# A graph layer's front reordered: node features, W1 and W3 first, table rows ahead of the dst check, edge attributes behind the rows

## The chip, the cores and the metric

The kernel runs on one core of a Trainium2 chip. The metric is the device time of one execution in microseconds (us); lower is better. A core has five engines that run their own instruction streams: TensorE (PE in the profile, PEld its weight loads), VectorE (DVE), ScalarE (ACT), GpSimd (POOL) and SyncE (SP, which only issues transfers). Transfers are issued by SP, ACT and POOL on queues of their own and are carried by 16 DMA engines that all queues share.

## The reference

1250 nodes have 512 features each: 384 are a vector part (128 channels of 3 components), 128 a scalar part s. 40000 edges, sorted by their target node dst, carry three attributes and a weight r. Two rounds of messages follow, then a residual and a layer norm:

```
x_j = x[src];  v_j, s_j = x_j[:, :384] as (E,128,3), x_j[:, 384:]
s_j = silu(s_j @ W1 + b1) @ W3 + b3
split = s_j * (rbf(r) * cutoff(r) @ W2 + b2)         # 3 x 128
v_msg = v_j * s1 + s3 * edge_attr;   msg = [v_msg, s2]
x1 = x + segment_sum(msg, dst)
... second round: v = x1_j @ U, v_V = v @ V, norms, a two-layer gate, segment_sum over dst
out = layernorm(x + x2)
```

`silu(s @ W1 + b1) @ W3 + b3` and its product with v depend on the node alone, so the kernel computes them once for each of the 1250 nodes, not for each of the 40000 edges.

## The kernel before

Nodes are kept in 10 blocks of 128 rows (NB = 10), shifted by a margin of 8. The edges are cut into 79 chunks of 512, four chunks to a group, 20 groups; a batch is one tile of 128 edges from each of the four chunks of a group, 81 batches in all.

**The front** (lines 118 to 381) loads everything and writes a table `table1` with one row of 640 numbers for each node to HBM. Its order is written out by hand: `manual_schedule` keeps the instructions of each engine in the order of the source. Its steps are:

- Memsets on DVE and POOL, iotas on POOL (`diff`, `part`, `lane`, `half_n`).
- Loads. ACT's queue brings the scalar columns of all nodes (`load_all_nodes`, line 192: blocks 1 to 4, blocks 5 to 8, then blocks 0 and 9 in two pieces each), POOL's queue the other 384 columns (line 203) and then W2, b2, U, V and the second gate's weights. SP's queue brings dst, b3, bu2, W1, b1, W3, weight, src and the edge attributes, in this order. Eight completion semaphores are handed round among the transfers of SP and ACT, and a transfer that takes over one waits until the transfer that had it has landed. Behind its transfers ACT loads its table for silu and runs one element through it (`warm`, line 194).
- The dst check (lines 277 to 290): DVE subtracts from each chunk the start of its window (`local_r`) and takes minimum and maximum, PE adds up the chunks that miss their window into `missed`, and DVE writes `missed_i`. Line 383 loads it into every engine, and a branch picks `windowed` (all chunks fit; taken here) or `general`.
- The layers. `turn_s` transposes the scalar part of four blocks on PE and copies it to `s_t` on DVE; `inner_layer` multiplies with W1 on PE (line 322) and applies silu on ACT. This goes by blocks 0 to 3, 4 to 7, and 8 and 9.
- `split_bias` (line 358) splits a bias into three bf16 parts on DVE, once for b3, once, at the end, for bu2.
- The rows. `make_rows` has PE add the bias and multiply with W3 (lines 336 and 337); `table_row` (line 577) has ACT copy 256 of the 384 results, DVE multiply the node's vector part with the rest (line 579), and SP store the row block (line 584).
- `make_sources` turns src by `by_tile` (four transposes on PE, a copy on ACT) into the index list `src_i` of the gathers.

**The loop** (`windowed`) first turns weight and attributes by `by_tile` and makes the first basis (lines 1459 to 1470). Then it runs the batches. For each, POOL gathers four tiles of 128 table rows by indirect transfers (`gather`, line 739), three batches ahead; the gathers go round five rooms of memory, three in `more`, two in `nodes`. From the fourth batch on the first gather of a batch waits for PE's edge factors two batches earlier. PE makes edge factors (line 854), DVE multiplies rows and factors (`messages`, lines 812 to 883), ACT marks the sources, PE adds the messages up and counts links between nodes. The second round is done by node blocks in between, and an end part normalizes the rows.

The loop's tiles lie in the memory that the front's tiles leave. So POOL's first loop tile, `number` (line 655), waits until the front's last work on DVE is done.

Of the kernel before, what the change touches and what calls it, by code (L numbers as in the profile page):

```python
# [11 lines left out]
F32 = mybir.dt.float32  # L12
# [52 lines left out]
def gnn_resnorm(  # L65
# [64 lines left out]
    rest = n_edges - full * CHUNK  # L130

# [10 lines left out]

    bias_f = front.tile([BIAS_ROWS - 1 + 32, V + 2 * C], F32, name="bias_f")
    nc.vector.memset(bias_f, 0.0)

    unfilled = full // 32 * 32
    nc.vector.memset(sh.att_r[unfilled:, :], 0.0)

# [7 lines left out]


# [4 lines left out]
    load_edges(dst_r, dst)  # L162
    first_last = slice(0, 3, 2)
    three = bias_f.rearrange("(r q) f -> r q f", q=32)[:, 0, :]
    nc.sync.dma_start(three[:, :V], b3.rearrange("(o f) -> o f", o=1).to_broadcast([3, V]))
    for h in range(2):
        nc.sync.dma_start(
            three[:, V + h * C : V + (h + 1) * C],
            bu2.rearrange("(h o c) -> h o c", o=1, c=C)[2 * h].to_broadcast([3, C]),
        )  # L170

    sh.nodes = const.tile([P, NB * width], F32, name="nodes")
    sh.xt = sh.nodes.rearrange("p (b f) -> p b f", f=width)
# [6 lines left out]
    last = n_nodes + MARGIN - (NB - 1) * P  # L180
    warm = const.tile([P, 1], F32, name="warm")
    nc.vector.memset(warm, 0.0)
    nc.vector.memset(sh.xt[last // 32 * 32 :, NB - 1, :], 0.0)
    nc.vector.memset(sh.xt[:MARGIN, 0, :], 0.0)
# [7 lines left out]
    load_all_nodes(nc.scalar, slice(V, width))  # L192

    nc.scalar.activation(warm, warm, AF.Silu)

    diff = front.tile([P, P], I32)
    nc.gpsimd.iota(diff, pattern=[[1, P]], base=0, channel_multiplier=-1)
    nc.gpsimd.memset(sh.src_r[unfilled:, :], 0.0)
    nc.gpsimd.memset(sh.wgt_r[unfilled:, :], 1.0)
    part = numbers([P, 1], [[0, 1]], 0, 1, "part")  # L200
    lane = numbers([P, P], [[1, P]], 0, 0, "lane")
    half_n = numbers([P, N_RBF], [[1, N_RBF]], 1, 0, "half_n")
    load_all_nodes(nc.gpsimd, slice(0, V))

    def load(engine, ap, shape, name):
        t = const.tile(shape, F32, name=name)
        engine.dma_start(t, ap)
        return t

    sh.h_t = const.tile([C, NB * P], F32, name="h_t")
    sh.w1_sb = load(nc.sync, w1, [C, C], "w1_sb")
    sh.b1_sb = load(nc.sync, b1.rearrange("(p o) -> p o", o=1), [C, 1], "b1_sb")

    sh.w3_sb = load(nc.sync, w3, [C, V], "w3_sb")
    load_edges(sh.wgt_r, edge_weight)
    load_edges(sh.src_r.bitcast(I32), src)
    load_edges(sh.att_r, edge_attr, 3)

    w2_sb = const.tile([P, V + CARRY], F32)
    nc.vector.memset(w2_sb, 0.0)
    for i in range(GROUP):
# [12 lines left out]
    sh.b3, sh.bu2 = b3, bu2  # L236


    ident = const.tile([P, P], F32)
    nc.vector.tensor_scalar(ident, diff, 0.0, None, op0=ALU.is_equal)  # L240
    share = front.tile([NCP, 1], F32)
    nc.vector.tensor_scalar(
        share, part[:NCP, :], float(SHARE), float(-MARGIN), op0=ALU.mult, op1=ALU.add
    )
    ones = const.tile([P, P], F32)
    nc.vector.memset(ones, 1.0)
    sh.ones_r = const.tile([BIAS_ROWS, P], BF16, name="ones_r")
    nc.vector.tensor_copy(sh.ones_r, ones[:BIAS_ROWS, :])
    nc.vector.tensor_scalar(half_n, half_n, 0.5, None, op0=ALU.mult)
    sh.ones, sh.ident, sh.lane, sh.part, sh.half_n = ones, ident, lane, part, half_n  # L250


# [9 lines left out]
    nc.vector.tensor_scalar(w2_sb[:, V:], lane[:, :CARRY], own, None, op0=ALU.is_equal)  # L262
# [13 lines left out]

    local_r = front.tile([NCP, CHUNK], F32)
# [10 lines left out]
    missed = ps_front.tile([1, 1], F32)  # L288
    nc.tensor.matmul(missed, misses, ones[:NCP, 0:1], start=True, stop=True)
    nc.vector.tensor_copy(missed_i, missed)  # L290


    sh.carried = fields.tile([P, NGR, TPC * CPG, CARRY], F32, name="carried")
    sh.attr, sh.local = sh.carried[:, :, :, :3], sh.carried[:, :, :, 3]
    sh.weight = fields.tile([P, NGR, TPC * CPG], F32, name="weight")
    sh.src_i = fields.tile([P, NGR, TPC * CPG], I32, name="src_i")
    sh.src_f = fields.tile([P, NGR, TPC * CPG], F32, name="src_f")

    def by_tile(ps, t, col, per, to, bufs=2):
        tp = ps.tile([P, TPC, P], F32, name="tp", bufs=bufs)  # L300
        view = t.rearrange("c (i e k) -> c i e k", i=TPC, k=per)
        for i in range(TPC):
            nc.tensor.transpose(tp[:, i, :NCP], view[:, i, :, col], ident[:NCP, :NCP])
        nc.scalar.copy(
            to.rearrange("p g (i j) -> p i g j", i=TPC),
            tp[:, :, :NCP].rearrange("p i (g j) -> p i g j", j=CPG),
        )


    s_ts = []  # L310

    def turn_s(b0, n):
        tp = ps_front.tile([P, 4 * P], F32, name="xs", bufs=2)
        for b in range(n):
            nc.tensor.transpose(tp[:, b * P : (b + 1) * P], sh.xt[:, b0 + b, V:], ident)
        s_t = front.tile([C, 4 * P], F32, name="s_t", bufs=3)
        nc.vector.tensor_copy(s_t[:, : n * P], tp[:, : n * P])
        s_ts.append(s_t)

    def inner_layer(s_t, b0, n):  # L320
        hp = ps_front.tile([C, 4 * P], F32, name="pp", bufs=4)
        nc.tensor.matmul(hp[:, : n * P], sh.w1_sb, s_t[:, : n * P], start=True, stop=True)
        nc.scalar.activation(
            sh.h_t[:, b0 * P : (b0 + n) * P], hp[:, : n * P], AF.Silu, bias=sh.b1_sb
        )

    sh.by_tile = by_tile
    by_tile(ps_front, local_r, 0, 1, sh.local, 1)
    sh.table1 = tc.dram_tile([NB * P, V + 2 * C], F32, name="table1")
    sh.table2 = tc.dram_tile([NB * P, width], F32, name="table2")  # L330

    def make_rows(b0, n):
        row = sh.rooms[b0 // 4]
        for b in range(b0, b0 + n):
            pp = ps_front.tile([P, 4 * P], F32, name="pp", bufs=4)[:, :V]
            nc.tensor.matmul(pp, sh.ones_r, sh.bias[:, :V], start=True, stop=False)
            nc.tensor.matmul(
                pp, sh.h_t[:, b * P : (b + 1) * P], sh.w3_sb, start=False, stop=True
            )
            table_row(nc, sh, pp, b, row[:, b - b0, :])  # L340

    def make_sources(step):
        if step == 0:
            nc.vector.tensor_scalar(
                sh.src_r, sh.src_r.bitcast(I32), float(MARGIN), None, op0=ALU.add
            )
            return
        by_tile(ps_front, sh.src_r, 0, 1, sh.src_f, 1)
        nc.vector.tensor_copy(sh.src_i, sh.src_f)

    spans = [(b0, min(4, NB - b0)) for b0 in range(0, NB, 4)]
    for span in spans[:-1]:
        turn_s(*span)
    inner_layer(s_ts[0], *spans[0])

    sh.bias = const.tile([BIAS_ROWS, V + 2 * C], BF16, name="bias")

    def split_bias(cols):
        left = bias_f[:BIAS_ROWS, cols]
        nc.vector.tensor_copy(sh.bias[:, cols], left)  # L360
# [1516 lines left out]
```

## Time and profile before

| | us |
|---|---|
| median of 3 runs | 502.84 |
| the three runs | 499.98, 502.84, 510.46 |
| the profiled execution | 500.5 |
| its span, first to last instruction | 498.7 |
| busy in it: DVE | 441.4 |
| PE | 410.5 |
| ACT | 369.1 |
| POOL | 348.6 |

A profile's times count from the start of the span. A line of the timeline has start, duration, engine (SPq, ACTq, POOLq are issues of transfers), line of the kernel, operation, and what is written from what; an x and a number behind it count merged instructions, whose duration is then the whole stretch; brackets hold the idle time ahead of it and what ended it. A line of the groups has count, busy us, mean ns of one, and idle time ahead with its releasers. A line of the queues has packets, MB and the share of the 16 DMA engines' time. What ended an idle time is inferred: of several things waited for the one that came last is named, and where that had long been done it was another, often a transfer.

### The profile page before, as it was taken

The numbers are of one execution on the slowest core, as the hardware profiler recorded it, in microseconds if no ns is written. First come the engines' busy times: TensorE is split into PE (matmuls) and PEld (weight loads), VectorE is DVE, ScalarE is ACT, GpSimd is POOL, SyncE is SP. The second block draws the span as 40 slices with busy tenths as digits, with TensorE's granted clock in tenths as the row PEclk, the third lists the DMA queues.
The fourth block names the chain that finished last, engine by engine and source line by source line (L and its number), as shares of the span: only waits on it lengthen the run. The fifth ranks groups of instructions, "written<-read, shape, count | busy, mean of one in ns | idle before, by whom it ended". The sixth has DMA issues, their size and how long they took to land. (4 is left out here: it accounts for less than half of the span.)

```text
span 498.7 us, 11033 instructions
## 1 busy us (share of the span) xinstructions
PE 410.5 (82%) x4193; PEld 226.0 (45%) x4193; DVE 441.4 (89%) x698; ACT 369.1 (74%) x941; POOL 348.6 (70%) x369
## 2 busy tenths in 40 slices
PE   2946777886889876898899799989979989998991
PEld 1522333353445344454445445544544554545780
DVE  6789998989988998999899799999978989987693
ACT  1436776597778979677898688998978798873573
POOL 6457777777777777777777777777776777655910
PEclk9966887999988999898999799999979999999996
DMA  8768888888888878888988988888887898889023
GB/s 244 252 219 248 256 264 253 263 288 265 263 252 293 258 227 300 252 246 256 297 293 241 312 255 284 294 285 294 263 288 242 270 293 283 272 258 344 2 107 109
DMA packets 38323, 126.96 MB, mean 255 GB/s; under 512 B 6689, under 2 KB 8239, under 8 KB 38259
## 3 DMA queue, kind: packets, MB, share of 16 engines
q0 software_dynamic: 26016, 104.86, 66.9%
q1 hardware_dynamic: 10910, 20.64, 11.8%
q10 hardware_dynamic: 1332, 0.64, 0.5%
q8 instruction: 35, 0.57, 0.4%
q14 instruction: 30, 0.24, 0.2%
HBM read 114.78 MB, written 11.34 MB: 253 GB/s over the span
## 5 line engine op out<-in xcount | busy, mean ns | idle before, releaser
L745 POOL DMA_INDIRECT more<-table,src_i x189 | 186.4, 986 | 59.6 <-issue 49.1
L745 POOL DMA_INDIRECT nodes<-table,src_i x124 | 124.3, 1002 | 42.3 <-issue 32.9
L845 ACT ACTIVATE one<-one,weight,src_f 128x128 f16<-128x128 f16 x313 | 128.5, 482 | 0.5 <-DVE magic L723 0.2
L854 PE MATMUL eb<-w_sb,basis_t 25*128 25x388 f32 x626 | 80.6, 574 | 55.3 <-DVE more L868 33.1
L835 ACT ACTIVATE one<-number,low 128x128 f16<-128x128 f16 x313 | 99.7, 392 | 4.2 <-PE adj L925 3.5
L868 DVE TENSOR_TENSOR more<-more,eb 128x1536 f32<-128x1536 f32 (+2 forms) x49 | 82.8, 1691 | 0.0
L865 DVE TENSOR_TENSOR more<-more,eb 128x1024 f32<-128x1024 f32 (+2 forms) x49 | 57.7, 1179 | 9.4 <-DMA more<-table,src_i 9.2
L854 PEld LDWEIGHTS eb<-w_sb,basis_t 25*128 25x128 f32 x626 | 26.4, 191 | 76.4 <-DVE more L868 45.1
L900 PE MATMUL agg<-more,hot 128*32 128x512 f32 (+1 forms) x378 | 58.8, 679 | 0.0
L868 DVE TENSOR_TENSOR nodes<-nodes,eb 128x1536 f32<-128x1536 f32 (+1 forms) x32 | 54.4, 1699 | 0.0
L907 PEld LDWEIGHTS agg<-more,spread 128*32 128x32 f32 x1134 | 35.9, 117 | 35.8 <-issue 35.5
L865 DVE TENSOR_TENSOR nodes<-nodes,eb 128x1024 f32<-128x1024 f32 (+1 forms) x32 | 37.9, 1185 | 7.1 <-DMA nodes<-table,src_i 6.8
L907 PE MATMUL agg<-more,spread 128*32 128x128 f32 x1134 | 43.8, 284 | 0.0
L823 DVE TENSOR_TENSOR spread<-hot,eb 128x384 f32<-128x384 f32 (+1 forms) x81 | 43.3, 535 | 0.0
L883 DVE TENSOR_TENSOR pair<-number,column 128x640 f16<-128x640 f16 (+1 forms) x81 | 38.7, 479 | 0.0
L925 PE MATMUL adj<-pair,one 128*128 128x160 f16 x313 | 35.8, 236 | 0.0
L900 PE MATMUL agg<-nodes,hot 128*32 128x512 f32 x248 | 34.9, 619 | 0.0
L812 DVE TENSOR_TENSOR hot<-lane,eb 128x128 f32<-128x128 f32 (+1 forms) x81 | 22.6, 280 | 13.2 <-PE eb L854 12.4
L805 ACT COPY basis_t<-work 128x512 f32<-128x512 f32 x20 | 11.7, 585 | 28.4 <-PE work L800 28.4
L907 PEld LDWEIGHTS agg<-nodes,spread 128*32 128x32 f32 x744 | 22.5, 111 | 19.9 <-issue 19.9
L925 PEld LDWEIGHTS <-one 128*128 128x128 f16 x313 | 19.9, 98 | 16.2 <-issue 14.7
L907 PE MATMUL agg<-nodes,spread 128*32 128x128 f32 x744 | 27.0, 274 | 0.0
(258 smaller groups left out, 689.9 us busy)
## 6 DMA issues: line engine op xcount, KB each, us to landing
table<-more SPq DMA_DIRECT2D x10, 320.0 KB, 2.4
spilled<-begun SPq DMA_DIRECT2D x12, 256.0 KB
more<-table,src_i POOLq DMA_INDIRECT x189
more<-spilled SPq DMA_DIRECT2D x2, 1280.0 KB
resid<-h_t SPq DMA_DIRECT2D x9, 256.0 KB, 4.2
node_x<-in_x_dram SPq DMA_DIRECT2D x8, 256.0 KB, 5.3
nodes<-table,src_i POOLq DMA_INDIRECT x124
nodes<-in_x_dram POOLq DMA_DIRECT2D x2, 768.0 KB
```

The costliest lines, as they stand in the source:

```text
L745: got = nc.gpsimd.indirect_dma_start(out=rows_t[:n, j, :], out_offset=None, in_=sh.table1, in_offset=bass.IndirectOffsetOnAxis(ap=sh.src_i ...
L812: nc.vector.tensor_tensor(hots[t][:m, js, :], lane[:m, None, :WIN].to_broadcast(shape), eb[:m, js, V + 3 : V + 4].to_broadcast(shape), op= ...
L823: nc.vector.tensor_mul(spread[t][:m, js], hots[t][:m, js, None, :].to_broadcast(shape), eb[:m, js, V : V + 3, None].to_broadcast(shape),)
L835: nc.scalar.activation(onehots[t][:, j, :], number[:, :P], AF.Abs, bias=low[:, e : e + 1])
L845: nc.scalar.activation(one, one, AF.Relu, scale=less[:, e : e + 1], bias=worth[:, e : e + 1])
L854: made = nc.tensor.matmul(eb[:, j, : V + CARRY], turned[g][rows, i, :], sh.w2_sb[rows, :], start=True, stop=True,)
L865: nc.vector.tensor_mul(msg[:m, js, V:], msg[:m, js, V:], eb[:m, js, C:V])
L868: nc.vector.tensor_mul(msg[:m, js, :V].rearrange("p t (k c) -> p t k c", k=3), msg[:m, js, :V].rearrange("p t (k c) -> p t k c", k=3), eb[ ...
L883: nc.vector.tensor_tensor(pair[:m, js, :].rearrange("p t (l h) -> p t l h", h=2), number[:m, : PARTS * WIN].rearrange("p (l h) -> p l h", ...
L900: nc.tensor.matmul(agg[j * WIN : (j + 1) * WIN, :], hots[t][:m, j, :], msg[:m, j, :width], start=(i == 0), stop=False, skip_group_check=True,)
L907: nc.tensor.matmul(agg[j * WIN : (j + 1) * WIN, c * C : (c + 1) * C], spread[t][:m, j, c, :], msg[:m, j, width:], start=False, stop=(i == ...
L925: nc.tensor.matmul(to[:, :, at : at + WIN], one[:m, j, :], pair[:m, j, :].rearrange("e (p n) -> e p n", n=WIN), start=(i == 0 and j == js[ ...
```

## The change

- SP's order is W1, b1, b3, W3, dst, bu2, src, weight; then the ten row blocks are stored; the attributes load behind them.
- POOL starts its node loads ahead of the memset for weight, `lane` and `half_n`; the attributes' memset moves from DVE to POOL, behind the loads.
- `turn_s` takes blocks 1 to 4, 5 to 8, and 0 and 9, and its copy runs on ACT. `inner_layer` runs for blocks 1 and 2, then 3 and 4, then 5 to 8, then 0 and 9.
- The first bias split comes ahead of DVE's small work on `half_n`, `place` and `sel`.
- Rows are made as 1, 2; 3, 4, 5; 6; 7, 8; and 0, 9, with the layers between them. src and the dst check come on DVE behind row 8 and ahead of rows 0 and 9; `missed_i`, `src_i`, the last columns of `w2_sb` and the second bias split follow.

`split_bias` is called `part_bias` now, otherwise unchanged. The loop is the same, instruction for instruction. The diff, cut:

```diff
+    warm = const.tile([P, 1], F32, name="warm")
+    nc.vector.memset(warm, 0.0)
     bias_f = front.tile([BIAS_ROWS - 1 + 32, V + 2 * C], F32, name="bias_f")
     nc.vector.memset(bias_f, 0.0)
-    nc.vector.memset(sh.att_r[unfilled:, :], 0.0)
...
-    load_edges(dst_r, dst)
+    diff = front.tile([P, P], I32)
+    nc.gpsimd.iota(diff, pattern=[[1, P]], base=0, channel_multiplier=-1)
+    part = numbers([P, 1], [[0, 1]], 0, 1, "part")
+    nc.gpsimd.memset(sh.src_r[unfilled:, :], 0.0)
...
     load_all_nodes(nc.scalar, slice(V, width))
     nc.scalar.activation(warm, warm, AF.Silu)
+    load_all_nodes(nc.gpsimd, slice(0, V))
+    sh.w1_sb = load(nc.sync, w1, [C, C], "w1_sb")
+    sh.b1_sb = load(nc.sync, b1.rearrange("(p o) -> p o", o=1), [C, 1], "b1_sb")
...
+    nc.sync.dma_start(three[:, :V], b3.rearrange("(o f) -> o f", o=1).to_broadcast([3, V]))
+    sh.w3_sb = load(nc.sync, w3, [C, V], "w3_sb")
+    load_edges(dst_r, dst)
...
+    load_edges(sh.src_r.bitcast(I32), src)
...
     nc.gpsimd.memset(sh.wgt_r[unfilled:, :], 1.0)
+    nc.gpsimd.memset(sh.att_r[unfilled:, :], 0.0)
+    load_edges(sh.wgt_r, edge_weight)
     lane = numbers([P, P], [[1, P]], 0, 0, "lane")
     half_n = numbers([P, N_RBF], [[1, N_RBF]], 1, 0, "half_n")
...
+    def turn_s(blocks):
+        tp = ps_front.tile([P, 4 * P], F32, name="xs", bufs=2)
+        for k, b in enumerate(blocks):
+            nc.tensor.transpose(tp[:, k * P : (k + 1) * P], sh.xt[:, b, V:], ident)
+        n = len(blocks) * P
+        s_t = front.tile([C, 4 * P], F32, name="s_t", bufs=3)
+        nc.scalar.copy(s_t[:, :n], tp[:, :n])
+        return s_t[:, :n]
...
+    first_s, next_s = turn_s((1, 2, 3, 4)), turn_s((5, 6, 7, 8))
+    inner_layer(first_s[:, : 2 * P], (1, 2))
+    inner_layer(first_s[:, 2 * P :], (3, 4))
+    part_bias(slice(0, V))
...
+    make_rows((1, 2))
+    inner_layer(next_s, (5, 6, 7, 8))
+    make_rows((3, 4, 5))
+    rest_s = turn_s((0, 9))
+    make_rows((6,))
+    inner_layer(rest_s, (0, 9))
+    make_rows((7, 8))
+    nc.vector.tensor_scalar(sh.src_r, sh.src_r.bitcast(I32), float(MARGIN), None, op0=ALU.add)
+    by_tile(ps_front, sh.src_r, 0, 1, sh.src_f, 1)
     local_r = front.tile([NCP, CHUNK], F32)
     nc.vector.tensor_scalar(local_r, dst_r, share, None, op0=ALU.subtract)
...
+    make_rows((0, 9))
     nc.tensor.matmul(missed, misses, ones[:NCP, 0:1], start=True, stop=True)
     nc.vector.tensor_copy(missed_i, missed)
+    nc.vector.tensor_copy(sh.src_i, sh.src_f)
+    load_edges(sh.att_r, edge_attr, 3)
     by_tile(ps_front, local_r, 0, 1, sh.local, 1)
+    nc.vector.tensor_scalar(w2_sb[:, V:], lane[:, :CARRY], own, None, op0=ALU.is_equal)
+    part_bias(slice(V, V + 2 * C))
```

More of the change, by code (lines that the diff above doesn't have):

```diff
@@ L299, in by_tile @@
[L299 to L318, printed above, removed]
@@ L332, in make_rows @@
[L332 to L349, printed above, removed]
```

170 lines of the change are left out of this document (82 added, 88 removed).

## The prediction

> **What bounds the kernel now.** I read the page first, then the gather line with who waits for it, then the timeline of the first 45 us, because every edit lies ahead of the first message.
>
> ```profile
> span 498.7 us, 11033 instructions
> L745 POOL DMA_INDIRECT more<-table,src_i x189 | 186.4, 986 | 59.6 <-issue 49.1
> L745 POOL DMA_INDIRECT nodes<-table,src_i x124 | 124.3, 1002 | 42.3 <-issue 32.9
> ```
> ```profile
> L745 POOL DMA_INDIRECT more<-table,src_i x189: 918/946/1802, 31.0 to 433.7; - x189
> L745 POOL DMA_INDIRECT nodes<-table,src_i x124: 942/946/1805, 47.0 to 442.1; - x124
> ```
>
> The 313 gathers start at 31.0 and the last at 442.1. They are busy 310.7 us and idle 101.9 us, of which 82.0 is "issue", POOL's own gap between gathers. So POOL waits only some 20 us for others in 412: the loop is a chain of gathers, and a first gather that comes x earlier moves the end by about x. DVE moves along if its own start moves too. The end of the front (lines up to 381) therefore sets the gain.
>
> ```profile
> 25.22 1.47 DVE L579 TENSOR_TENSOR more<-nodes,pp 128x384 f32<-128x384 f32 x2 [0.18 <-ACT more L578]
> 27.99 0.42 DVE L365 TENSOR_TENSOR bias<-bias_f,bias 1x256 bf16<-1x256 f32 x1
> 28.54 0.33 POOL L655 IOTA number<- 128x256 f16 x1 [9.40 <-DVE bias L365]
> 31.05 1.05 POOL L745 DMA_INDIRECT more<-table,src_i  x1 [0.58 <-ACT carried L304]
> 34.66 0.69 DVE L788 TENSOR_TENSOR basis<-turn,fade 128x320 f32<-128x320 f32 x1
> 39.40 0.29 DVE L812 TENSOR_TENSOR hot<-lane,eb 128x128 f32<-128x128 f32 x1
> ```
>
> The last two table rows end on DVE at 26.69. The bias split behind them ends at 28.41 (27.99 + 0.42), 1.72 later, and that releases POOL: its first loop tile starts at 28.54 and the first gather 2.64 us after the split. I call that end F; here F = 28.41. DVE's first message follows 11.0 us after F. Both hang on F, not on the landing of the table.
>
> What comes ahead of the rows:
>
> ```profile
> 1.74 3.96 ACTq L413 DMA_DIRECT2D nodes<-in_x_dram  x4
> 2.09 0.52 POOL L199 MEMSET counts<- 16x512 f32 x1
> 3.06 1.77 POOL L407 DMA_DIRECT2D nodes<-in_x_dram  x2
> 5.74 1.28 ACT L194 ACT_TABLE_LOAD   x1 [5.74 <-DVE row_i L254]
> 7.03 0.20 ACT L194 ACTIVATE warm<-warm 128x1 f32<-128x1 f32 x1
> 9.52 0.19 PE L289 MATMUL missed<-ones,misses 80*1 80x1 f32 x2 [9.52 <-DVE misses L284]
> 13.03 3.51 PE L322 MATMUL pp<-s_t,w_sb 128*128 128x512 f32 x4 [0.89 <-DMA w_sb<-in_L_gnn_W_dram]
> 18.01 3.11 DVE L579 TENSOR_TENSOR more<-nodes,pp 128x384 f32<-128x384 f32 x4 [0.79 <-DMA w_sb<-in_L_gnn_b_dram]
> ```
>
> PE's first work waits 9.52 us for the dst check, its first layer waits for W1 until 13.03, and the first row is multiplied at 18.01. Those waits are what the edits remove.
>
> **The change, part by part.** Clock times below are on the scale of this execution.
>
> *Loads.* W1, b1, b3, W3 go first on SP's queue, ahead of dst; bu2, src and weight follow. W1 is then issued first of all, beside ACT's loads and before POOL's traffic, so it is no longer what the layer waits for. The dst check's 9.52 goes too: PE's first work is the transposes.
>
> *What is late next: ACT.* s_t is now copied by ACT, behind its DMA issues, the table load and warm. Those end at 7.23 (7.03 + 0.20) and were covered while PE waited; now they lie on the path. ACT's last issue (to 5.70) waits for node blocks 5 to 8 to land. POOL's loads of the other 384 columns move ahead of L199's memset and two iotas, by some 0.8 us (2.09 to 3.06, less one small iota that stays), so their data come that much earlier, into the tail of that load:
>
> ```profile
> q10 hardware_dynamic: 804, 0.40, 37.1%
> ```
> ```profile
> q10 hardware_dynamic: 1200, 0.59, 45.9%
> q0 software_dynamic: 13, 0.06, 15.7%
> ```
> ```profile
> q0 software_dynamic: 354, 1.50, 83.6%
> q1 hardware_dynamic: 4, 0.00, 0.1%
> ```
>
> These are the queues from 0 to 4 us, from 0 to 5, and from 5 to 10. ACT's queue (q10) had moved 0.40 MB at 4 us and 0.59 at 5; POOL's (q0) began just before 5. From 5 to 10 POOL's queue moved 354 packets and SP's (q1) four. A POOL packet holds an engine 0.19 us (83.6% of 16 engines for 5 us, over 354). Starting near 4 us, POOL finds about 0.19 MB of 512-byte packets left, some 23 for each engine. Call ACT's delay d. Lower end 0: they finish undisturbed. Upper end: one POOL packet ahead of each, 23 x 0.19 = 4.4 us for what took 1, d = 3.4. I take 1.7, the middle, which is nearest to one POOL load going in between (768 KB at 1.50 MB per 354 packets are 181, 11 for each engine, 2.1 us).
>
> The Trainium skill's DMA: Bandwidth & Descriptors, section "Queues, rings and completion order", says that each engine goes round robin between the queues, a packet at a time. By fair turns SP would not have had 4 packets against 354, so this trace doesn't bear out fair turns; taken literally here it gives the upper end, 3.4.
>
> *Layers and rows.* The prices:
>
> ```profile
> L322 PE MATMUL pp<-s_t,w_sb x6: 377/938/1193, 13.0 to 20.1; 128*128 128x512 f32 x4, 128*128 128x256 f32 x2
> L315 PE MATMUL xs<-ident,nodes x10: 273/421/422, 10.2 to 16.5; 128*128 128x128 f32 x10
> 17.41 0.33 PE L336 MATMUL pp<-bias,ones_r 65*128 65x384 bf16 x1
> 17.57 0.81 PE L337 MATMUL pp<-w_sb,h_t 128*128 128x384 f32 x2
> 17.60 0.37 ACT L578 COPY more<-pp 128x256 f32<-128x256 f32 x1 [0.34 <-PE pp L337]
> L805 ACT COPY basis_t<-work 128x512 f32<-128x512 f32 x20 | 11.7, 585 | 28.4 <-PE work L800 28.4
> ```
>
> PE starts at about half speed: a transpose took 421 ns early and 273 at 16.4, and a 512-column pass 0.88 early (3.51 / 4) against 0.43 by the later rows. For a row costs 0.81 there ((3.11 - 0.67) / 3 on DVE, which PE feeds), 0.16 of it the bias pass (17.41 to 17.57), which leaves 0.65 for two passes of 384. PE was fast 3.3 us after it began unbroken work at 13.03. A slow row is estimated at twice, 1.62. The Trainium skill, in TensorE: Matmul & The Clock Gate, Part 1, tells of a free-running window of some 3.4 us that must be busy before the clock opens, which agrees, and by which the point can fall up to one window later; that is a rival below.
>
> The path with d = 1.7: ACT free at 8.93; first s_t copy 0.59 gives 9.52; the two two-block layers, four slow 256-column passes of 0.44, 11.28; row 1 slow, row 2 fast (3.3 us after 9.52 is 12.8), 13.71; the four-block layer, 0.87, 14.58; rows 3 to 6 and two transposes, 3.24 + 0.22, 18.04; layer of blocks 0 and 9, 0.43, and rows 7 and 8, 1.62, 20.09; hand-over, ACT's copy and the multiply, 0.20 + 0.37 + 0.67, so row 8 ends on DVE at 21.33. Rows are paced by PE, so DVE's half_n, place and sel work, moved behind the first bias split, is covered: a dozen operations like L262's 0.23 below, ahead of a first row at 13.4.
>
> *dst check.* It was free in the wait for the loads; now it stands between row 8 and rows 0 and 9 on DVE:
>
> ```profile
> 7.31 0.47 DVE L278 TENSOR_SCALAR local_r<-dst_r,share 80x512 f32<-80x512 int32 x1
> 9.31 0.16 DVE L284 SCALAR_TENSOR_TENSOR misses<-ends 80x1 f32<-80x1 f32 x1
> 21.04 0.41 DVE L344 TENSOR_SCALAR counts<-counts 80x512 f32<-80x512 int32 x1
> 24.73 0.30 DVE L349 CAST src_i<-src_f 128x320 int32<-128x320 f32 x1
> 6.33 0.23 DVE L262 TENSOR_SCALAR w_sb<-lane,own 128x4 f32<-128x4 f32 x1
> 9.75 0.15 DVE L290 CAST missed_i<-missed 1x1 int32<-1x1 f32 x1 [0.28 <-PE missed L289]
> ```
>
> 0.41 for src and 2.16 for the check (7.31 to 9.47) bring DVE to 23.90; rows 0 and 9, already made by PE, 1.40 (2 x 0.67 and gaps), 25.30; missed_i, src_i and the w2 columns, 0.15 + 0.31 + 0.23, 25.99; the bias split, 1.72 as before, F = 27.7. Every engine's branch now waits for missed_i at 25.5, where POOL and PE branched early; DVE's comes last, after F, as it did, so this costs nothing.
>
> *att behind the rows.* Issued at about 25.7 (SP's last row goes first).
>
> ```profile
> b_sb<-in_L_gnn_b_dram SPq DMA_DIRECT2D x1, 0.5 KB, 7.8
> table<-more SPq DMA_DIRECT2D x10, 320.0 KB, 2.4
> 30.21 1.28 ACT L304 COPY carried<-tp 128x320 f32<-128x320 f32 x2
> 32.30 0.46 ACT L779 ACTIVATE turn<-turn 128x320 f32<-128x320 f32 x1
> ```
>
> From landing, three transposes with their copies and ACT's sine take about 3.8 us before DVE's basis can start; basis came 6.25 us after F. So att costs nothing if it lands by F + 2.45 = 30.2. A 320 KB store took 2.4 us; 468 KB at the same rate 3.5, landing 29.2. Covered by 1.0. The far row is b1's 7.8, landing 33.5: DVE 3.3 late, of which the gathers, three batches ahead, would feel a part.
>
> **The sum.** F moves from 28.41 to 27.7, -0.7 us, and the end with it: 500.5 becomes 499.8 (span 498.7 plus the 1.8 around it). The three runs shown have a median of 502.84, 2.3 above the profiled execution (lowest 499.98). The forecast of a median is 502.84 - 0.7 = 502.1. With d from 0 to 3.4 F runs from 26.0 to 29.4, -2.4 to +1.0.
>
> **Rivals.** (1) Clean start: blocks 5 to 8 land as early as before, d = 0. For it: q10 was at 0.59 MB by 5 us, and dst no longer shares it. Against: POOL's packets come 0.8 earlier. -2.4: 498.1 for such an execution, 500.4 as a median. (2) Slower, one mechanism: POOL's earlier loads share the engines with blocks 5 to 8, ACT waits with its issue, and table load and s_t copies queue behind it. It turns into a loss when d is over 2.4. At d = 3.4 it is +1.0, and with PE fast two rows later than 3.3 us, +1.6, it is +2.6: 503.8 to 505.4. For it: 354 packets against 4. (3) att lands at 33.5: -0.7 + 3.3, less what POOL's lead absorbs, up to +2.6, 505.4. Against: the queue is nearly empty by then. (4) The rows come early but nothing follows, since F is set by DVE's list: that is largely my forecast, for 4.6 us of earlier rows (13.4 against 18.0) shrink to 0.7 by the check, PE's slow start and the interleaved layers.
>
> **How the numbers follow.** Forecast (within about 1 of -0.7) 45%, rival 1 25%, rival 2 22%, rival 3 6%, else 2%. The range takes rival 1 on the profiled execution's base, 498.0, and the upper end of rivals 2 and 3 on the median, 505.5. Two per cent is 10 us, about what a measurement of this kernel can tell from no change, and no case reaches it: faster 0.03, same 0.92, slower 0.05.
>
> **What would show it.** ACT's table load at 7 to 8 instead of 5.7 confirms d; at 5.7, rival 1. First table-row multiply on DVE near 13 instead of 18.0; the two-block layer passes in the slow group and most row passes in the fast; DVE's check between row 8 and row 0; the end of the second bias split near 27.7; the first gather 2.6 behind it; no DVE wait ahead of basis. I am wrong if the first gather moves by over 2.5 us, if att is waited for, or if the loop's length (first gather to last, 411) changes by more than the shift.

## The result, and the profile after

The changed kernel's median is 495.64 us (six executions, 494.26 to 500.08), that of the kernel before beside it 502.15 (six, 499.98 to 510.46). The ratio is 0.9892, with an interval of 0.9852 to 0.9931: 5.4 us less, between 3.5 and 7.4. That is within 2 per cent, but the forecast was 502.1 with a range from 498.0, so it was too high and its range did not hold. The profiled execution is the slowest of the six (500.08, span 498.3). In this ratio and all below, executions that fell into a disturbed state are left out, so a ratio is not always that of the two medians beside it.

The timeline of the changed kernel, from ACT's loads of blocks 1 to 8 to DVE's first message (start, duration, engine, line, what is written from what, and in brackets the idle time with what ended it):

```profile
0.74 1.01 ACTq L398 DMA_DIRECT2D nodes<-in_x_dram  x2
...
5.52 1.28 ACT L190 ACT_TABLE_LOAD   x1 [5.52 <-DMA nodes<-in_x_dram]
6.82 0.20 ACT L190 ACTIVATE warm<-warm 128x1 f32<-128x1 f32 x1
7.55 2.08 PE L277 MATMUL pp<-s_t,w_sb 128*128 128x256 f32 x4 [1.27 <-ACT s_t L271]
9.74 1.49 PE L306 MATMUL pp<-w_sb,h_t 128*128 128x384 f32 x2
11.34 1.49 PE L306 MATMUL pp<-w_sb,h_t 128*128 128x384 f32 x2
11.67 0.67 DVE L570 TENSOR_TENSOR more<-nodes,pp 128x384 f32<-128x384 f32 x1 [1.06 <-ACT more L569]
12.62 1.44 PE L277 MATMUL pp<-s_t,w_sb 128*128 128x512 f32 x2
14.06 0.81 PE L306 MATMUL pp<-w_sb,h_t 128*128 128x384 f32 x2
...
19.33 1.47 DVE L570 TENSOR_TENSOR more<-nodes,pp 128x384 f32<-128x384 f32 x2 [0.57 <-ACT more L569]
23.05 0.16 DVE L358 SCALAR_TENSOR_TENSOR misses<-ends 80x1 f32<-80x1 f32 x1
23.16 1.26 DVE L570 TENSOR_TENSOR more<-nodes,pp 128x384 f32<-128x384 f32 x2
24.35 0.14 DVE L365 CAST missed_i<-missed 1x1 int32<-1x1 f32 x1
25.30 0.54 SPq L139 DMA_DIRECT2D counts<-in_edge_attr_dram  x1
26.15 0.42 DVE L292 TENSOR_TENSOR bias<-bias_f,bias 1x256 bf16<-1x256 f32 x1
26.78 0.34 POOL L646 IOTA number<- 128x256 f16 x1 [5.97 <-DVE bias L292]
29.23 1.04 POOL L736 DMA_INDIRECT more<-table,src_i  x1 [0.38 <-DMA counts<-in_edge_attr_dram]
29.78 1.31 PE L255 MATMUL tp<-ident,counts 80*128 80x80 f32 x8 [3.39 <-DMA counts<-in_edge_attr_dram]
33.18 0.69 DVE L779 TENSOR_TENSOR basis<-turn,fade 128x320 f32<-128x320 f32 x1 [0.95 <-ACT turn L770]
38.61 0.29 DVE L803 TENSOR_TENSOR hot<-lane,eb 128x128 f32<-128x128 f32 x1 [0.68 <-PE eb L845]
```

ACT's table load starts at 5.52, against 5.74 before. The first row is multiplied at 11.67 instead of 18.01. The end on DVE that the prediction calls F comes at 26.57 (26.15 + 0.42) instead of 28.41, the first gather at 29.23 instead of 31.05, DVE's first message at 38.61 instead of 39.40.

The gathers of the changed kernel, by their line (shortest, median and longest in ns, then first and last start):

```profile
L736 POOL DMA_INDIRECT more<-table,src_i x189: 945/949/1796, 29.2 to 433.0; - x189
L736 POOL DMA_INDIRECT nodes<-table,src_i x124: 943/949/1657, 45.7 to 441.6; - x124
```

From first to last gather it is 412.3 us, 1.3 more than before. So this profile shows 1.8 us at the start, most of it given back in the loop, and the median shows 5.4. The experiments had to say which of the two stands for the change, and why the start moved by more than 0.7.

### The profile page after: what moved, and what is told of

The parts are those of the page before. It is cut to its first block, busy times and chain, and to the rows that moved or that the text cites. A ratio compares the mean times of both kernels' runs of the same rounds, so it can differ in the third digit from the quotient of the medians.

```text
span 498.3 us, 11039 instructions
## 1 busy us (share of the span) xinstructions
PE 410.3 (82%) x4195; PEld 225.5 (45%) x4195; DVE 439.4 (88%) x694; ACT 371.8 (75%) x945; POOL 352.5 (71%) x370
## 3 DMA queue, kind: packets, MB, share of 16 engines
HBM read 114.78 MB, written 11.34 MB: 253 GB/s over the span
## 5 line engine op out<-in xcount | busy, mean ns | idle before, releaser
L736 POOL DMA_INDIRECT more<-table,src_i x189 | 188.8, 999 | 59.3 <-issue 50.1
L845 PE MATMUL eb<-w_sb,basis_t 25*128 25x388 f32 x626 | 79.5, 566 | 57.1 <-DVE more L859 32.9
L891 PE MATMUL agg<-more,hot 128*32 128x512 f32 (+1 forms) x378 | 57.3, 663 | 0.0
L891 PE MATMUL agg<-nodes,hot 128*32 128x512 f32 x248 | 36.3, 642 | 0.0
L796 ACT COPY basis_t<-work 128x512 f32<-128x512 f32 x20 | 11.7, 587 | 23.3 <-PE work L791 23.3
```

The source lines that it names most:

```text
L736: got = nc.gpsimd.indirect_dma_start(out=rows_t[:n, j, :], out_offset=None, in_=sh.table1, in_offset=bass.IndirectOffsetOnAxis(ap=sh.src_i ...
L845: made = nc.tensor.matmul(eb[:, j, : V + CARRY], turned[g][rows, i, :], sh.w2_sb[rows, :], start=True, stop=True,)
L891: nc.tensor.matmul(agg[j * WIN : (j + 1) * WIN, :], hots[t][:m, j, :], msg[:m, j, :width], start=(i == 0), stop=False, skip_group_check=True,)
```

## Experiments

The theories that the expectations name:

- **start**: the end moves with the first gather; all else is the spread of the loop between executions.
- **loop**: the change also shortens the loop itself in most executions.
- **messages**: DVE's first message sets the end, so the wait for the attributes costs time.
- **lead**: late attributes give POOL more lead over DVE, which shortens the loop.
- **delay** (the prediction's) and **clean start** (its first rival): POOL's earlier node loads hold up ACT, or don't.

Each set ran on one chip, beside the kernel before. In two of the six sets (that of the result and the one called third below) the whole took some 500 us, in the others 578 to 593 (last section), so only kernels of one set are compared.

### First set: both kernels again, the attributes, and a front made longer

Kernel `before_again` is the kernel before, `after_again` the changed kernel, neither with an edit.

> The kernel before, unchanged. It shows how far two sets of runs of one kernel lie apart. Both theories: ratio 1.000, interval within 0.995 to 1.005; first gather at 31.0, end of the second bias split at 28.4. If its interval reaches 0.99, a single comparison of this kernel can't carry a gain of 1%, and the measured 6.5 us below 502.1 are partly the draw of the runs.

> The changed kernel, unchanged. Theory start (the end moves with the first gather, which came 1.8 us earlier, and the rest of the measured 5 us is the loop's own spread between runs): with more runs the gain shrinks to 1.8 us, ratio 0.9964, about 500. Theory loop (the changed front also shortens the loop by some 3 us in most executions, and the profiled one was an exception): ratio 0.989 again, about 496 to 497, and this profile has a loop of about 408 us from first to last gather instead of 412.3.

`att_ahead`:

```diff
-    load_edges(sh.att_r, edge_attr, 3)
-    load_edges(sh.wgt_r, edge_weight)
+    load_edges(sh.wgt_r, edge_weight); load_edges(sh.att_r, edge_attr, 3)
```

> The changed kernel with the attributes loaded behind weight, ahead of the stored rows, as before. It takes away the 1.0 us that DVE's basis waited for ACT's sine. Theory start (POOL's gathers alone set the end): the wait was not on the path; first gather and time as the changed kernel's, within 1 us, unless the 468 KB delay the rows. Theory messages (DVE's first message sets the end, 38.6 against 39.4 before): message at 37.6, time 1 us less. Theory lead (late attributes give POOL 1 us more lead over DVE, and this shortens the loop): the time goes up by 2 to 3 us.

`front_plus4` (added work that nothing reads):

```diff
+    idle = front.tile([P, 512], F32, name="idle")
+    for _ in range(8):
+        nc.vector.memset(idle, 0.0)
     part_bias(slice(V, V + 2 * C))
```

> The changed kernel with eight fills of 512 columns on DVE, some 3.9 us, ahead of the second bias split; nothing reads what they write. Theory start: the first gather comes 3.9 us later, at 33.1, and the time is 3.9 us above the changed kernel's, ratio to the kernel before 1.004 if the changed kernel's is 0.996. Theory loop: the loop's length doesn't hang on the start, so again 3.9 more, but from 0.989: ratio 0.997. If the end doesn't move one for one with the front, both fall.

The kernel before had a median of 578.23 here.

| | first gather | median | ratio to before |
|---|---|---|---|
| before_again | 32.00 | 577.64 | 0.9998 (0.9968 to 1.0028) |
| after_again | 29.38 | 576.18 | 0.9962 (0.9928 to 0.9995) |
| att_ahead | 29.29 | 577.11 | 0.9965 (0.9930 to 1.0001) |
| front_plus4 | 33.14 | 583.17 | 1.0094 (1.0054 to 1.0133) |

The kernel before is itself again within 0.3 per cent. The change gains 2.2 us where its first gather comes 2.6 earlier, as theory start has it. Eight fills cost 7 us for 3.8 of a later gather, which is more than one for one (the intervals leave 3 to 12). The two kernels with early and with late attributes have the same first gather and the same time, though DVE's first message came at 37.13 with the early ones and at 39.20 with the late ones: the attributes are waited for, and no cost of the wait shows. That is against messages and lead, though intervals of 2 us leave room for a part of either.

### Second set: a start put back, and the attributes alone

`after_third` is the changed kernel again.

> The changed kernel once more, since two sets of runs disagree (ratio 0.9892 and 0.9962, and the second set had a loop of 482 to 488 us where the first had 411). Theory start: the gain is the 1.8 to 2.6 us by which the first gather comes earlier, ratio 0.995 to 0.9965 in any set. Theory loop: where the loop is short (about 411 us from first to last gather, 500 us in all), the ratio is 0.989 again; where it is long, 0.996.

`front_plus2` has `range(4)` in place of `range(8)` above.

> The changed kernel with four fills of 512 columns on DVE ahead of the second bias split, which in the run with eight cost 0.66 each: 2.6 us, so the first gather is back at the kernel before's 31.5 to 32. Theory start: ratio 1.000, within 0.003. Theory loop (something of the change beside the first gather's time shortens the loop): the ratio stays 0.003 to 0.006 below 1.

`before_att_late` is the kernel before with one part of the change:

```diff
-    load_edges(sh.att_r, edge_attr, 3)
-    split_bias(slice(V, V + 2 * C))
+    load_edges(sh.att_r, edge_attr, 3); split_bias(slice(V, V + 2 * C))
```

> The kernel before with one part of the change alone: the attributes load behind the stored rows. Theory start: the first gather stays at 31 to 32 (it may gain a few tenths, since 468 KB less share the DMA engines with the table's inputs), DVE's basis waits 1 to 2 us, and the ratio is 1.000. Theory lead (late attributes give POOL more lead over DVE, which shortens the loop): ratio 0.993.

`att_mid`:

```diff
-    make_rows((0, 9))
+    load_edges(sh.att_r, edge_attr, 3); make_rows((0, 9))
-    load_edges(sh.att_r, edge_attr, 3)
```

> The changed kernel with the attributes' load one step earlier on SP's queue, ahead of the stores of rows 0 and 9 instead of behind them, issued at about 21 instead of 24.9. It should land by 26.5, so the transposes aren't waited for and DVE's first message comes 1 to 2 us earlier than in the changed kernel, at 37 to 38. Theory start: the first gather is as in the changed kernel (29.3) and so is the time. Theory messages: 1 to 2 us less than the changed kernel.

| | first gather | median | ratio to before (589.93) |
|---|---|---|---|
| after_third | 28.16 | 589.04 | 0.9871 (0.9799 to 0.9942) |
| front_plus2 | 30.39 | 587.73 | 0.9960 (0.9921 to 0.9999) |
| before_att_late | 31.14 | 586.72 | 0.9968 (0.9917 to 1.0018) |
| att_mid | 29.87 | 587.78 | 0.9968 (0.9930 to 1.0006) |

This set is inconclusive: 3 us of first gather show nothing in the medians, and in the ratios nothing beyond their intervals; that of `after_third` rests on three executions. `front_plus2` put the first gather at 30.39, not at the 31.5 to 32 that its expectation counts on. Late attributes alone are at 0.9968, with an interval that holds both theories' 1.000 and 0.993. `att_mid` misses its expectation: the attributes, issued at 20.65 ahead of the last two row stores, came in time, but the first gather then waited 1.66 us and came later (29.87 against 28.16). The likely reason is that the last row lands behind the attributes.

### Third set: the short loop

`after_fourth` is the changed kernel, `att_ahead_2` and `front_plus4_2` are the kernels above.

> The changed kernel, to stand beside the next three on one chip. Theory start: where the loop is short (411 us from first to last gather), ratio 0.995 to 0.9965. Theory loop: 0.989. Where the loop is long (480 to 500), both 0.996, as in the sets before.

`gaps_filled`:

```diff
+    part_bias(slice(V, V + 2 * C))
     make_rows((1, 2))
+    local_r = front.tile([NCP, CHUNK], F32)
+    nc.vector.tensor_scalar(local_r, dst_r, share, None, op0=ALU.subtract)
...
     inner_layer(next_s, (5, 6, 7, 8))
...
-    local_r = front.tile([NCP, CHUNK], F32)
-    nc.vector.tensor_scalar(local_r, dst_r, share, None, op0=ALU.subtract)
...
-    make_rows((0, 9))
+    load_edges(sh.att_r, edge_attr, 3); make_rows((0, 9))
...
-    load_edges(sh.att_r, edge_attr, 3)
...
-    part_bias(slice(V, V + 2 * C))
```

What moves behind row 2 is the whole dst check on DVE, to `misses`.

> The changed kernel with DVE's waits between the table's rows filled: the second bias split moves ahead of row 1 (1.8 us off the end), the dst check behind row 2 (2.2 us off the end), and the attributes' load ahead of the stores of rows 0 and 9. DVE stood idle some 3.5 us between 11.7 and 20.1, so rows 0 and 9 should end on DVE near 22.5 instead of 24.4 and the front at 23.0 instead of 26.6. The first gather then waits for the last row's landing or for POOL's four fills: 25.5 to 26.5 instead of 29.3, 2.8 to 3.8 us earlier. Theory start: the time is 2.8 to 3.8 us below the changed kernel's where the loop is short. If the loop does not follow its start, nothing beyond 1 us.

> The changed kernel with the attributes loaded ahead of the stored rows, again. In the first set it brought DVE's first message 2.1 us earlier than the changed kernel (37.1 against 39.2), with the same first gather (29.3), and the time stayed (0.9965 against 0.9962). Theory start: the same here, within 0.2 per cent of the changed kernel. Theory messages: 1 to 2 us less. Theory lead: 2 to 3 us more.

> The changed kernel with eight fills on DVE ahead of the second bias split, again: the first gather comes 3.8 us later. Theory start where the loop is short: 3.8 us, 0.8 per cent, above the changed kernel. In the long loop it was 7 us above, 1.3 per cent, with an interval from 0.5 to 2 per cent.

| | first gather | median | ratio to before (501.41) |
|---|---|---|---|
| after_fourth | 28.27 | 497.97 | 0.9945 (0.9914 to 0.9975) |
| att_ahead_2 | 29.27 | 498.11 | 0.9889 (0.9841 to 0.9936) |
| gaps_filled | 32.79 | 502.40 | 1.0025 (0.9990 to 1.0059) |
| front_plus4_2 | 34.02 | 503.43 | 1.0056 (1.0017 to 1.0095) |

Here the medians follow the first gather: 4.5 us later cost 4.4, and 5.75 cost 5.5. On this line the kernel before, with the first gather at 31.05 of its first profile, belongs at 500.7; its median is 501.41. Each first gather is that of one profile, and the changed kernel's varies by 1.5 us from profile to profile (below), so the line holds to about that. The change gains 2.8 us by the ratio (1.3 to 4.3), 3.4 by the medians, for 2.8 us of an earlier first gather. Theory start holds where the loop is short, and the 0.989 that theory loop expected lies outside this interval. `att_ahead_2`, its ratio taken over four executions, has a lower ratio and the same median as the changed kernel, so on the attributes it decides nothing more.

`gaps_filled` was meant as a better kernel and is slower than the changed one by 0.8 per cent. Its timeline says why:

```profile
5.12 1.40 SPq L202 DMA_DIRECT2D bias_f<-in_L_gnn_bu_dram  x2
13.63 0.29 DVE L287 CAST bias<-bias_f 65x256 bf16<-65x256 f32 x1 [3.01 <-DMA bias_f<-in_L_gnn_bu_dram]
15.51 1.24 DVE L569 TENSOR_TENSOR more<-nodes,pp 128x384 f32<-128x384 f32 x2
...
25.78 1.16 SPq L574 DMA_DIRECT2D table<-more  x2
26.48 0.14 DVE L366 CAST missed_i<-missed 1x1 int32<-1x1 f32 x1
28.22 0.34 POOL L645 IOTA number<- 128x256 f16 x1 [8.97 <-DMA table<-more]
32.79 1.04 POOL L735 DMA_INDIRECT more<-table,src_i  x1 [2.66 <-DMA node_x<-in_x_dram]
```

The bias split stood ahead of row 1 and waited for bu2, two transfers of 1.5 KB issued by 6.5 that landed at 13.6; DVE was idle for 3.01 us and row 1 came at 15.51. DVE's last front work was done at 27.0, but POOL's first loop tile came at 28.22, 1.6 after `missed_i` (26.62), and PE's first loop work came beside it, at 28.30: so here the branch released it, most likely, and not DVE's end. And the first gather waited 2.66 more; the releaser that is named had been issued at 30.15 and is none of its inputs, so what it waited for is likely the last row, stored at 26.6 behind 468 KB of attributes.

The rows of `after_fourth` show why the same kernel's first gather is at 28.27 here and at 29.23 in the first profile:

```profile
11.24 0.84 PE L306 MATMUL pp<-w_sb,h_t 128*128 128x384 f32 x2
12.52 0.67 DVE L570 TENSOR_TENSOR more<-nodes,pp 128x384 f32<-128x384 f32 x1 [0.28 <-ACT more L569]
25.05 0.42 DVE L292 TENSOR_TENSOR bias<-bias_f,bias 1x256 bf16<-1x256 f32 x1
28.27 1.04 POOL L736 DMA_INDIRECT more<-table,src_i  x1 [0.48 <-DMA counts<-in_edge_attr_dram]
```

PE's passes of row 2 took 0.84 here and 1.49 there (11.34 in the first fence): PE was at full speed one row and one layer earlier, and F came at 25.47 instead of 26.57. Over the five profiles of the changed kernel the first gather lies at 27.89, 28.16, 28.27, 29.23 and 29.38, mean 28.6; in the two of the kernel before at 31.05 and 32.00, mean 31.5. The change moves it by 2.9 us on the mean, 1.1 more than the first pair of profiles showed.

### Fourth set: POOL's place, and a start that comes earlier still

`after_fifth` is the changed kernel. `pool_late`:

```diff
-    load_all_nodes(nc.gpsimd, slice(0, V))
...
     nc.gpsimd.memset(sh.wgt_r[unfilled:, :], 1.0)
-    nc.gpsimd.memset(sh.att_r[unfilled:, :], 0.0)
...
     half_n = numbers([P, N_RBF], [[1, N_RBF]], 1, 0, "half_n")
+    load_all_nodes(nc.gpsimd, slice(0, V))
+    nc.gpsimd.memset(sh.att_r[unfilled:, :], 0.0)
```

`fills_early` gives `number` and `basis` memory of their own, written at the end of POOL's front work, and moves two fills behind the gathers of the first three batches:

```diff
+    sh.number = const.tile([P, LOW], F16, name="number")
...
+    sh.basis = const.tile([P, TPC * CPG, FEAT], F32, name="basis")
...
         for t in range(min(ahead, NT)):
             gather(t)
+        nc.gpsimd.memset(sums[1][P - WIN :, :], 0.0)
+        nc.gpsimd.memset(node_x, 0.0)
```

`both_early` has that too, and moves the dst check, src and the second bias split:

```diff
     make_rows((1, 2))
+    local_r = front.tile([NCP, CHUNK], F32)
...
     inner_layer(next_s, (5, 6, 7, 8))
     make_rows((3, 4, 5))
+    nc.tensor.matmul(missed, misses, ones[:NCP, 0:1], start=True, stop=True)
     rest_s = turn_s((0, 9))
     make_rows((6,))
+    nc.vector.tensor_scalar(sh.src_r, sh.src_r.bitcast(I32), float(MARGIN), None, op0=ALU.add)
     inner_layer(rest_s, (0, 9))
+    nc.vector.tensor_copy(missed_i, missed)
+    part_bias(slice(V, V + 2 * C))
     make_rows((7, 8))
```

> The changed kernel, to stand beside the next three on one chip. First gather at 28.2 or 29.3, by whether PE's clock is full at the second row. Theory start: ratio 0.994 to 0.996 where the loop is short.

> The changed kernel with one part undone: POOL's node loads start behind the memset for weight and the two iotas again, about 0.9 us later. Theory delay, the prediction's: POOL's packets hold up blocks 5 to 8, so ACT's table load starts earlier than the 5.3 to 5.6 of the changed kernel, by up to 0.9, and the first gather with it. Theory clean start, its first rival: ACT's table load stays at 5.3 to 5.6, POOL's columns land later, and the time stays within 1 us.

> The changed kernel with two of POOL's four loop fills ahead of the front's end: number and basis get memory of their own and are written in the front, where POOL stands idle; sums and node_x are filled behind the gathers of the first three batches. The first gather then waits for the index list, the branch and the last row's landing instead of for the front's last DVE work and 2.4 us of fills: 26.6 to 27.2 instead of 28.2 to 29.3, some 2 us earlier, of which the two fills behind the gathers give back 1.2 if POOL has no wait there. Theory start: time 1 to 2 us less than the changed kernel where the loop is short. If the loop is paced by DVE's first message, which doesn't move: no change.

> The changed kernel with the fills as in the run before, and on DVE the dst check behind row 2, src behind row 6 and the second bias split ahead of row 7 (in the run with DVE's gaps filled, the bias split stood ahead of row 1 and waited 3 us for bu2, and the branch waited for a late count of misses; here both come when their inputs are there). The rows end at 23.5 to 24 instead of 24.4, the front's last DVE work at 24.8 instead of 26.6, DVE's first message 1.5 to 2 us earlier, the first gather at 26.2 to 26.8. Theory start: 2 to 3 us less than the changed kernel where the loop is short.

| | first gather | median | ratio to before (589.46) |
|---|---|---|---|
| after_fifth | 27.89 | 585.65 | 0.9933 (0.9895 to 0.9971) |
| pool_late | 28.52 | 585.53 | 0.9939 (0.9901 to 0.9978) |
| fills_early | 27.61 | 588.26 | 0.9994 (0.9957 to 1.0032) |
| both_early | 28.17 | 584.41 | 0.9913 (0.9869 to 0.9957) |

Two fences, `after_fifth` first, then `pool_late`: POOL's first loads and ACT's table load.

```profile
2.19 1.77 POOL L398 DMA_DIRECT2D nodes<-in_x_dram  x2
5.36 1.28 ACT L190 ACT_TABLE_LOAD   x1 [5.36 <-DMA nodes<-in_x_dram]
```
```profile
3.12 1.77 POOL L398 DMA_DIRECT2D nodes<-in_x_dram  x2
5.35 1.28 ACT L190 ACT_TABLE_LOAD   x1 [5.35 <-DMA nodes<-in_x_dram]
```

POOL starts 0.93 us later, and ACT starts at the same time to 0.01. The delay theory is refuted: POOL's place shows no effect on ACT beyond the 0.36 us by which its table load varies anyway (5.27 to 5.63). The queues say why. In the first profile of the changed kernel, from 0 to 5 us, ACT's (q10) and POOL's (q0):

```profile
q10 hardware_dynamic: 1200, 0.59, 40.6%
q0 software_dynamic: 5, 0.02, 1.9%
```

ACT's queue had moved these 1200 packets by 4.75 us, when POOL's had moved none. Before, POOL's had moved 13 by 5 us, though its first load was issued 0.87 us later there (3.06 against 2.19). The earlier issue brought POOL's data no earlier than in the kernel before, so its packets never met these 1200.

`fills_early` and `both_early` took F out of the way, and the first gather hardly moved. In `fills_early`:

```profile
19.55 4.06 SPq L583 DMA_DIRECT2D table<-more  x3
23.71 0.38 SPq L137 DMA_DIRECT2D counts<-in_edge_attr_dram  x1
25.00 0.41 DVE L300 TENSOR_TENSOR bias<-bias_f,bias 1x256 bf16<-1x256 f32 x1
27.61 1.04 POOL L739 DMA_INDIRECT more<-table,src_i  x1 [6.86 <-ACT fade L681]
```

POOL had been idle for 6.86 us, and ACT's `fade` is no input of a gather. The last row's store is the third of the first line, 0.32 long, so issued at 23.3: 4.3 us from there to the gather. In the first profile of the changed kernel the last four stores, by their tile, were issued from 20.0 to 24.5:

```profile
L575 SPq DMA_DIRECT2D table<-more x4: 319/320/478, 20.0 to 24.5; - x4
```

That is 4.7 us to its gather at 29.23. Where the 468 KB of attributes had been issued ahead of that store, the stretch was longer: 6.1 us in `att_mid` (23.8 to 29.87), 6.2 in `gaps_filled` (26.6 to 32.79). So a second limit, most likely the landing of the last row (these traces have no time for it), stands within a few tenths behind F, and a front that ends earlier on DVE alone wins no more. The times agree with that for `both_early`; that `fills_early` is 0.6 per cent slower than `after_fifth`, at the edge of the intervals, isn't explained.

### Fifth set: the dst check put back

`check_first`, the whole check with `missed` and `missed_i`:

```diff
+    load_edges(dst_r, dst)
     sh.w1_sb = load(nc.sync, w1, [C, C], "w1_sb")
...
-    load_edges(dst_r, dst)
...
+    local_r = front.tile([NCP, CHUNK], F32)
...
+    nc.vector.tensor_copy(missed_i, missed)
     assert NB == 10
     first_s, next_s = turn_s((1, 2, 3, 4)), turn_s((5, 6, 7, 8))
```

`both_early_2` is `both_early` again.

> The changed kernel with one part undone: dst loads first on SP's queue, and the dst check runs on DVE and PE ahead of the transposes, as before. PE then waits until about 9.5 for the count of misses, ACT's first copy of s_t comes at 11 instead of 6.9, and the first row at 14.5 to 15.5 instead of 11.6; but the 2.2 us of the check are no longer between row 8 and row 0. Theory by the sum: front's end 1 to 1.5 us later than the changed kernel's, first gather 29.5 to 30.5, time 1 to 1.5 us more. Rival: rows are paced by PE and DVE's later work hides in them, so the whole 3 us of the later first row reach the end: first gather 31 to 32, as in the kernel before.

> The kernel with fills, dst check, src and second bias split moved ahead, again. In the first set its first gather waited for the last row's landing, 4.9 us after that row's store was issued, and started at 28.2, so nothing was won on the changed kernel (0.9913 against 0.9933). Theory start: the same here, ratio 0.991 to 0.996. If DVE's earlier end counts by itself: 2 us less than the changed kernel, 0.990 or below where the loop is short.

| | first gather | median | ratio to before (592.56) |
|---|---|---|---|
| check_first | 33.54 | 594.12 | 1.0065 (1.0015 to 1.0114) |
| both_early_2 | 28.75 | 584.12 | 0.9867 (0.9808 to 0.9927) |

`check_first`, from its timeline:

```profile
5.54 0.43 SPq L153 DMA_DIRECT2D w_sb<-in_L_gnn_W_dram  x1
7.62 0.19 PE L321 MATMUL missed<-ones,misses 80*1 80x1 f32 x2 [7.62 <-DVE misses L316]
8.89 0.59 ACT L271 COPY s_t<-xs 128x512 f32<-128x512 f32 x1 [1.64 <-PE xs L268]
14.17 1.55 PE L306 MATMUL pp<-w_sb,h_t 128*128 128x384 f32 x2 [1.41 <-DMA w_sb<-in_L_gnn_W_dram]
33.54 1.04 POOL L736 DMA_INDIRECT more<-table,src_i  x1 [0.39 <-DMA counts<-in_edge_attr_dram]
```

The check itself delays the layers by 2 us (s_t at 8.89 instead of 6.9). The rows are delayed by 4.5, for a reason that neither theory had: W3, issued at 5.54 instead of 2.56, landed at 14.2, 8.6 us later. It was issued late because dst's two transfers went first and SP then waited 1.7 us for dst to land. From 6 to 8 us the queues of POOL (q0) and SP (q1) moved:

```profile
q0 software_dynamic: 170, 0.72, 93.2%
q1 hardware_dynamic: 16, 0.00, 0.4%
```

In the changed kernel row 1's pass started at 9.74 without a wait for W3. So the order on SP's queue is worth at least as much as the check's place, and the rival's 31 to 32 was too mild. `both_early_2` again has the last row's landing ahead of its first gather (store issued at 23.9, gather at 28.75). Its 0.9867, from four executions, lies below the range that theory start gave, with an interval that reaches into it. The changed kernel didn't run beside it here; in the one set that ran both they are not told apart, 0.9913 against 0.9933.

## Why the prediction was wrong

- **What bounds the kernel: right, in the short loop.** 313 gathers in a chain; the median follows the first one, 4.4 us for 4.5 and 5.5 for 5.75. First gather to last is 411.0 before and 411.1, 411.4 and 411.9 in three kernels of the third set, though 412.3 in the changed kernel's first profile and 406.9 in `front_plus4_2`: one execution's loop says little to a few us.
- **"A first gather that comes x earlier moves the end by about x", and F + 2.64: right.** Measured F + 2.66 (26.57 to 29.23). What the step left out is, most likely, the last row's landing: where nothing else kept POOL, the first gather came 4.3 to 5.3 us behind that store's issue (`fills_early`, `both_early`), a close second already.
- **ACT's delay d = 1.7: the step that failed.** "Starting near 4 us, POOL finds about 0.19 MB of 512-byte packets left": it found none, for its first packets came only after 4.75 us, no earlier than in the kernel before, and ACT's 1200 had been moved by then. So d was 0. ACT's table load came at 5.27 to 5.63 in the five profiles, 5.74 and 6.06 in the two before, and the same with POOL 0.93 later. Whether POOL's packets would go ahead of ACT's if they met was not tried. `check_first` and `gaps_filled` show whom POOL's bulk does reach, transfers of SP that are issued behind it: from 6 to 8 us POOL's queue moved 170 and 155 packets and SP's 16 and 17, with W3 in the one and bu2 in the other still to land. The Trainium skill's DMA: Bandwidth & Descriptors, section "Queues, rings and completion order", has round-robin turns, a packet at a time, which taken literally gave the upper end of d, with one packet of the profile to a turn. The page's packet holds several descriptors, so the profile's need not be the same thing; ACT's transfers were no test of it, and 170 against 16 doesn't look like equal turns.
- **PE's slow start: mis-sized the other way.** I had one slow row. PE turned fast between the four-block layer and row 3 in the first profile (two slow rows and a slow layer, 1.44 for its two passes against 0.87), and after row 1 in `after_fourth`. That gave back 0.8 of the 1.9 which d had cost in the sum (ACT free at 7.02 against 8.93, F at 26.57 against 27.7) in the one and nothing in the other. The free-running window in TensorE: Matmul & The Clock Gate, Part 1, of the Trainium skill makes the point shift between executions of one kernel, as it does here; the 500 ns either way that the page gives for the shift is less than the 2 us measured.
- **dst check, src and second bias split on DVE: right.** 23.21 for the check's end against 23.90, and from there to F 3.36 against 3.8.
- **att: landed later than forecast, and cost nothing.** PE could take it at 29.78, 3.2 behind F, and DVE's basis waited 0.95. I had said that a landing behind F + 2.45 costs time; that was wrong: `att_ahead` shows the same time with the message 2.1 us earlier. POOL's lead of three batches would explain that; it was not tried apart.
- **Rival 1** (d = 0, -2.4) was the right case: F at 26.0 against 25.2 to 26.7 measured, and a shift of the first gather of 2.9 on the mean of the profiles. In the set of the result it would have given 502.15 - 2.4 = 499.8. Rival 2 is refuted, rival 3's landing at 33.5 didn't come (29.78), rival 4 described the size wrongly with the forecast.
- **The rest of the 5.4 us is not settled.** Of the 4.7 us between the forecast change and the measured one, d explains 1.7. The five sets with the changed kernel give 0.9892, 0.9962, 0.9871, 0.9945 and 0.9933; weighed by their intervals that is about 0.993, some 3.4 us of 500, near the 2.9 of the first gather. So the set of the result lies some 2.6 us on the lucky side of what the other short-loop set showed (0.9945). A loop that the change itself shortens is not excluded by fractions of a per cent, but no profile of the short loop shows one (411.0 us before, 412.3 and 411.1 after).

## What to carry to other kernels

Ahead of a long chain, find every condition of its first link (here the last work on DVE, the landing of the last row, the branch) and forecast the latest; moving one alone stops at the next a few tenths later. Small transfers that something early needs go ahead of the bulk on every queue: issued behind POOL's bulk and SP's own larger loads, 192 KB took 8.6 us and 1.5 KB took 7. And where a single execution's loop varies by some us, a forecast of a fraction of a per cent needs a range for the draw of the runs as well as for the mechanism.

## What was not expected of the hardware

In four of the six sets, each on another chip, the kernel before took 578 to 593 us instead of 500. DVE's busy time is the same (441 us in both), PE's is 449.8 us against 410.5 in the first profiles; the gathers wait. From the waits of the kernel before, first as in the table of times (498.7), then as `before_again` (574.5), columns total us, times and longest:

```profile
POOL nodes L745 <- PE eb L854: 3.6, 3, 1.8
POOL more L745 <- PE eb L854: 2.3, 2, 1.9
```
```profile
POOL more L745 <- PE eb L854: 28.5, 22, 2.5
POOL nodes L745 <- PE eb L854: 22.0, 13, 3.1
```

There the gathers wait 50.5 us for PE's edge factors instead of 5.9, and from first to last gather it is 484.9 us instead of 411.0. The granted clock is 0.884 against 0.934. Why PE's part comes late on those chips was not tried. In that long loop the end follows its start only loosely: even the stretch behind the last gather, 56.5 to 56.7 us in the profiles of the short loop, is 57.5 to 64.5 there. That is why the second and fourth set decide little about a few us.
